# Four residual convolution layers on one core: the first tile's input norm by quarters, the first tile of two later stages by halves and earlier, the last three tiles' offset on another engine

## The chip, the core and the metric

The kernel runs on one core of a Trainium2 chip. A core has five engines that run their own instruction streams in order and wait for one another by semaphores: PE (matrix products into PSUM), DVE (VectorE), ACT (ScalarE), POOL (GpSimd) and SP, which here only issues transfers. Sixteen DMA engines move data between the memory of the chip and the core's own memory. The metric is the device time of one execution in microseconds (us); times of several runs are given by their median. One execution is recorded by the hardware profiler, and all rows below come from it.

## The reference

A batch of 8192 images of 8 channels, 16x16, goes through four layers, each of the form x = x + layer(group_norm(x)) with 4 groups:

```
x = x + L0(_gn(x))   # tensor-train operator of three cores over (8, 16, 16), and a bias
x = x + L1(_gn(x))   # 3x3 convolution, then a batch norm over the whole batch, then relu
x = x + L2(_gn(x))   # 3x3 convolution of values rounded to 8 bits; the scale is the largest |value| of the batch
x = x + L3(_gn(x))   # 3x3 convolution with weights reduced to their sign, edge padding, and a bias
```

L1 needs the mean and variance of its output over the whole batch, and L2 the largest absolute value of its input over the whole batch. So the batch is gone through three times.

## The kernel before

The batch is cut into 64 tiles (NT) of 128 images. A tile is a matrix of 128 partitions (8 channels x 16 rows) by 2048 columns (128 images x 16 columns of a picture) of f32, 1 MB. Three stages follow one another.

**Stage 1** (0 to about 2785 us): layer 0 and the convolution of layer 1. Each tile is loaded twice: as `xb` in a layout whose partitions hold a picture's column and part of the image's number, into one of three buffers `bs`, and as `xt` in the tile layout, into one of four buffers `xs`. The norm of the input works on `xb`: ACT squares it (`norm_b_square`), DVE sums values and squares over rows (`norm_b_sums`), a transpose and five small operations give mean and variance (`group_stats`; its last step, a power of -0.5, is on POOL), a second transpose spreads the result (`norm_b_spread`), and DVE subtracts and multiplies into a buffer `xn` (`norm_b_apply`). Then PE multiplies by the third core (`expand`: tile `pu`, copied to `u` by ACT, two halves for each quarter of a tile) and by the product of the first two cores (`main`: tile `po`, one for each quarter; DVE then adds `po` to `xs`, which is called a drain here). The product of the first two cores is itself made once at the start: POOL spreads the first core into `c0x`, PE makes `cps`, ACT copies it to `core`. `add_bias` adds layer 0's bias to `xs` on POOL. After that come the norm and convolution of layer 1 for the tile before. A loop over the 256 quarters (`for n in range(NT * NQ)`) calls all of this; small constants for later layers (`late_constants`) are made by DVE between the first quarters. The small pack of constants (232 KB) and the large one (690 KB) are loaded from ACT's queue.

PSUM tiles `po`, `pm` and `pc` share three buffers (tag `mm`), so a new one waits until the one three before it has been drained.

**Stage 2** (about 2786 to 3230): for each tile the batch norm and relu of layer 1's output on ACT, `y`, its addition to `x` on POOL (`sum2`), squares on ACT (`square2`), sums by PE (`sums2`, tile `gs`), statistics on DVE and ACT (`stats2`), the power on POOL (`sigma2`), the statistics as rows for PE (`spread2`, tile `gb`), the subtraction of the mean on DVE and the store of the tile (`centre2`), and the running maximum (`range2`). `load2` loads `y` and `x` of a tile; the buffers of a tile's `y` are those of an earlier tile's, so a load waits until that tile's addition has read it. The first four tiles never leave the core's memory. In this stage and the next, tile i is the i-th in the stage's own order. The calls stand in one loop over i, in which tile i is at `sum2`, tile i-1 at `square2`, i-2 at the statistics and i-3 at `centre2`.

**Stage 3** (about 3231 to the end): layers 2 and 3. For a tile: scaling to 8 bits on DVE (`scale2`, `v`), conversion on ACT (`round2`, `q`), PE's convolution in two halves (`layer2`, tiles `pq`); half 0 is drained by DVE after `bias2` added the bias on ACT, half 1 by ACT into `ys` or `z` and an addition on POOL. Then squares (`square3`), sums by PE (`s`), statistics and power (`stats3`), rows (`rows3`, `rows_e`), PE's spreading (`ps_r` the factor, `ps_o` the offset), scaling on DVE (`scale3`), the split into a high part on ACT (`high3`, `hi`) and a low part on POOL (`low3`, `lo`), each with its edge columns copied by ACT (`edges`), PE's convolution of both (`layer3`, tiles `pf`, 24 matmuls), and DVE's last step (`finish`) before the store. `offset3` makes `c`, the offset with the bias, on ACT, and `low3` adds it to `x` on POOL after the low part. A loop over i calls these with shifts, so that tiles i-3 to i+3 are in work together.

**What sets the order.** PE, DVE, ACT and POOL are used through a wrapper that keeps the program's order on each engine; it records all of these instructions at its own line, L43, so that a row is told by its tiles and not by its line. `nc.sync.dma_start` stands outside it: SP issues in the order that the tile framework builds, and it waits in that order.

The rows name what they write and read (out<-in).

Of the kernel before, what the change touches and what calls it, by code (L numbers as in the profile page):

```python
# [8 lines left out]
F32 = mybir.dt.float32  # L9
F32R = mybir.dt.float32r  # L10
BF16 = mybir.dt.bfloat16
# [7 lines left out]
P = 128  # L19
# [4 lines left out]
R = 8  # L24
# [29 lines left out]
def tile_net(ctx: ExitStack, tc: tile.TileContext, xb, xt_in, pack0, pack1, out):  # L54
# [11 lines left out]
    def load_pack(src, parts, pool, name):  # L66
        t = pool.tile([P, src.shape[1]], F32, name=name)
        nc.scalar.dma_start(t, src)
        views, at = {}, 0
        for key, n in parts:  # L70
            views[key] = t[:, at:at + n]
            at += n
        return views
# [209 lines left out]
    with first as s:  # L283
# [24 lines left out]

        def add_bias(t):
            v = samples(T[t]["x"])  # L310
            pool.tensor_tensor(v, v, bias0_t.unsqueeze(1).to_broadcast([P, P, W]), ALU.add)

# [22 lines left out]

        def norm_b_apply(t, q=None):
            src = T[t]["xb"]
            if q in (None, 0):
                T[t]["xn"] = xns[t % 2]
            xn = T[t]["xn"]  # L340
            n = NB // 2 if q is None else NB // NQ
            for k, op, i in ((0, ALU.subtract, src), (1, ALU.mult, xn)):
                for a in range(0, NB, n) if q is None else [q * n]:
                    cols = slice(a, a + n)
                    dve.tensor_tensor(rows_b(xn)[:, cols], rows_b(i)[:, cols],
                                      spread0[:, k, cols].unsqueeze(2).to_broadcast([P, n, 32]), op)

# [147 lines left out]

        load_b(0)
        for t in range(min(3, NT)):
            if t + 1 < min(3, NT):
                load_b(t + 1)
            load_t(t)  # L500
        rest = late_constants(s.enter_context(tc.tile_pool(name="late", bufs=1)))
        next(rest)
        norm_b_square(0)
        norm_b_sums(0)
        c0x = ys[0][:, 0:C * C * H].rearrange("p (n m h) -> p n m h", n=C, m=C)
        pool.tensor_tensor(c0x, w0["c0"].rearrange("p (n m) -> p n m", n=C).unsqueeze(3).to_broadcast([P, C, C, H]),
                           shz[:, 1:H + 1].unsqueeze(1).unsqueeze(1).to_broadcast([P, C, C, H]), ALU.mult)
        norm_b_stats(0)
        cps = ps_u.tile([P, 2 * C, H * R], F32, name="cps", tag="pu")
        for n in range(C):  # L510
            pe.matmul(cps[:, n], c0x[:, n].rearrange("p m h -> p (m h)"), w0["c1"], start=True, stop=True)
        c01v = core01.rearrange("p s (n h) -> p n h s", n=C)
        for n in range(0, C, C // 2):
            act.copy(c01v[:, n:n + C // 2], cps[:, n:n + C // 2].rearrange("p n (h s) -> p n h s", s=R))
        if NT > 1:
            norm_b_square(1)
        norm_b_spread(0)
        for q in range(NQ):
            norm_b_apply(0, q)
            if q == 0:  # L520
                expand(0, 0, 0)
                expand(0, 0, 1)
                add_bias(0)
        if NT > 1:
# [140 lines left out]
    with tc.tile_pool(name="p2", bufs=2) as p2, tc.tile_pool(name="ps2", bufs=2, space=PSUM) as ps2:  # L665
# [14 lines left out]
        nc.vector.tensor_tensor(L["corr"], L["corr"], ksum, ALU.subtract)  # L680

        def sum2(i):
            x, y = T[i]["x"], T[i].pop("y")
            act.activation(y, y, AF.Relu, bias=bn_b, scale=bn_a)
            pool.tensor_tensor(x, x, y, ALU.add)

        def square2(i):
            T[i]["sq"] = p2.tile([P, F], F32, name=f"sq2_{i}", tag="sq2")
            act.activation(T[i]["sq"], T[i]["x"], AF.Square)

# [58 lines left out]
        for i in [*range(STAY), *range(BEGUN, free)]:  # L749
            on(i, load2)  # L750
        for i in range(NT + 4):
            if i == 1:
                on(free, load2)
            on(i + AHEAD2, lambda i: i <= free or load2(i))
            on(i, sum2)
            on(i - 2, sums2)
            on(i - 3, spread2)
            on(i - 1, square2)
            on(i - 2, stats2)
            on(i - 3, centre2)  # L760
            on(i - 2, sigma2)
            on(i - 3, range2)
# [18 lines left out]
    with ExitStack() as s:  # L781
# [53 lines left out]
        def round2(i):  # L835
            q = wk.tile([P, F], BF16, name=f"q_{i}", tag="q")
            act.copy(q, T[i].pop("v"))
            T[i]["q"] = q

        def bias2(i):  # L840
            x = halves(T[i]["x"])[:, 0]
            act.activation(x, x, AF.Identity, bias=L["bias2"], scale=1.0)

        def layer2(i, h):
# [6 lines left out]
            pc, x = pc.rearrange("p k n -> p (k n)"), halves(T[i]["x"])[:, h]  # L851
            if h == 0:
                dve.scalar_tensor_tensor(x, pc, inv, x, ALU.mult, ALU.add)
            else:
                z = z3[i % 2]
                act.activation(z, pc, AF.Identity, bias=L["bias2"], scale=inv)
                pool.tensor_tensor(x, x, z, ALU.add)
# [4 lines left out]
        def stats3(i):  # L862
# [4 lines left out]
            stats_pow(T[i]["mv"])  # L867

        def offset3(i):
            T[i]["c"] = small.tile([P, P], F32, name=f"c_{i}", tag="c")  # L870
            act.activation(T[i]["c"], o3, AF.Identity, bias=L["bias3"], scale=1.0)

        def scale3(i):
            x = T[i]["x"]
            t = t3[i % 2]
            for a, b in HALVES:
                dve.tensor_tensor(samples(t)[:, a:b], samples(x)[:, a:b], over_w(r3, a, b), ALU.mult)
            T[i]["t"] = t


# [8 lines left out]
        def low3(i):  # L889
            hi = T[i]["hi"]  # L890
            T[i]["lo"] = lo = wk.tile([P, P, W + 2], F32R, name=f"lo_{i}", tag="lo")
            pool.tensor_tensor(lo[:, :, 1:W + 1], samples(T[i].pop("t")), hi[:, :, 1:W + 1].bitcast(F32), ALU.subtract)
            x = samples(T[i]["x"])
            pool.tensor_tensor(x, x, over_w(T[i].pop("c"), 0, P), ALU.add)

        def edges3(i):
            edges(T[i]["lo"])

        def layer3(i, h):
            pc = ps_c.tile([P, 2, BANK], F32, name=f"pf_{i}_{h}", tag="pc")  # L900
            for m, t in enumerate(("hi", "lo")):
                for k in range(2):
                    q = 2 * h + k
                    tv = T[i][t][:, q * QS:(q + 1) * QS]
                    for n in range(3):
                        pe.matmul(samples(pc[:, k]), L["sign3"][:, n], tv[:, :, n:n + W],
                                  start=(m == n == 0), stop=(m == 1 and n == 2))
            T[i]["pf", h] = pc

# [14 lines left out]
        for i in range(-FIRST, NT + 4):  # L924
# [4 lines left out]
            at(i, square3)  # L929
            at(i + 1, layer2, 0)  # L930
            spread(i + FIRST, i - 1)
            at(i - 1, offset3)
            at(i + 1, layer2, 1)
            at(i + FIRST, scale2)
            at(i, stats3)
            at(i - 1, scale3)
            at(i - 2, edges3)
            at(i + 2, round2)
            at(i - 1, high3)
            at(i + 2, bias2)  # L940
            at(i - 1, low3)
            at(i - 2, layer3, 0)
            at(i - 2, finish, 0)
            at(i - 2, layer3, 1)

# [63 lines left out]
```

## Time and profile before

| | us |
|---|---|
| three runs, median | 4006.31 (4005.77 to 4006.53) |
| the profiled execution, its own time | 4004.3 |
| its span, first to last instruction | 4002.5 |
| mean granted TensorE clock | 0.963 of full speed |
| PE, DVE, ACT, POOL busy | 3771.8, 3386.6, 2380.6, 2580.2 |
| data moved | 564.48 MB |

The profile gives the busy time of each engine, a picture of the span in 40 slices, the chain of work that ended last (followed back from the last instruction to what released it), groups of instructions, and, for any window, a timeline of instructions with the idle time ahead of each and what ended it. A busy PE is not a PE at its peak, since matmuls are pipelined. Idle time of an engine off the chain costs nothing. By the 40 slices the DMA engines move 390 to 425 GB/s from slice 29 to 32, that is in stage 2, and 95 to 190 GB/s elsewhere.

### The profile page before, as it was taken

What the parts mean: (1) busy time and instruction counts of PE and PEld (TensorE: products, weight loads), DVE (VectorE), ACT (ScalarE), POOL (GpSimd) and SP (SyncE); (2) the same over time, 40 slices, a digit from 0 to 9 for tenths busy, and PEclk for the clock granted to TensorE, in tenths of its full rate; (3) what the DMA queues carried; (4) which work ended last, traced back from release to release, by engine and by line L of the source; (5) the groups of instructions that cost most, each with busy time, mean ns of one, the idle gap of its engine ahead of it and who ended that gap; (6) DMA issues with size and microseconds to landing.
All of it is one profiled execution on the core that took longest, in us unless ns stands there. A gap on an engine that the chain in (4) does not pass through costs nothing.

```text
span 4002.5 us, 55803 instructions
## 1 busy us (share of the span) xinstructions
PE 3771.8 (94%) x20296; PEld 2012.8 (50%) x20358; DVE 3386.6 (85%) x6311; ACT 2380.6 (59%) x2420; POOL 2580.2 (64%) x2597
## 2 busy tenths in 40 slices
PE   8999999999999999999999999998665569999998
PEld 4555555555555555555555555554221135555555
DVE  8888888888888888888888888885999889999997
ACT  4555555555555555555555555554665557777775
POOL 4555555555555555555555555544887759999999
PEclk9999999999999999999999999999777689999999
DMA  3222222222222222222222222213999914444432
GB/s 146 95 95 106 95 95 106 95 95 106 95 95 104 97 95 101 101 95 97 104 95 96 105 95 95 95 54 136 390 424 425 399 42 189 180 179 189 180 148 105
DMA packets 77458, 564.48 MB, mean 141 GB/s; under 512 B 8576, under 2 KB 8704, under 8 KB 8832
## 3 DMA queue, kind: packets, MB, share of 16 engines
q1 hardware_dynamic: 76896, 559.97, 35.8%
q8 instruction: 161, 2.64, 0.3%
q14 instruction: 113, 0.93, 0.1%
q10 hardware_dynamic: 288, 0.94, 0.1%
HBM read 314.47 MB, written 246.42 MB: 140 GB/s over the span
## 4 chain that ended last, share of the span: by engine, by line
PE 86%; DVE 6%; DMA 4%; issue 2%; POOL 1%; ACT 0%; POOLq 0%; DVEq 0%; SPq 0%; ACTq 0%
PE po L43 46%; PE pu L43 14%; PE pf L43 9%; PE pm L43 6%; PE pq L43 4%; PE s L43 3%; PE pc L43 3%; DVE top L43 2%; DMA yk<-y_d 1%; DMA x_d<-u 1%; DMA u<-x_d 1%; DMA x_d<-xs 0%; DMA xs<-x_d 0%; DVE u L43 0%; POOL xs L43 0%
## 5 line engine op out<-in xcount | busy, mean ns | idle before, releaser
L43 PE MATMUL po<-u,core 128*128 128x512 f32 (+1 forms) x4112 | 1895.6, 604 | 1.3 <-DVE xs L43 1.3
L43 ACT COPY u<-pu 128x2048 f32<-128x2048 f32 x512 | 955.6, 1866 | 773.1 <-PE pu L43 773.1
L43 PEld LDWEIGHTS po<-u,core 128*128 128x128 f32 x4112 | 739.8, 190 | 904.5 <-issue 870.4
L43 POOL TENSOR_TENSOR e<-x1n,x 128x512 f32<-128x512 f32 x250 | 302.4, 1209 | 574.7 <-ACT x L43 568.3
L43 PE MATMUL pu<-w,xn 32*128 32x256 f32 x8192 | 587.8, 401 | 4.9 <-DVE xn L43 2.8
L43 DVE TENSOR_TENSOR xs<-po,xs 128x512 f32<-128x512 f32 x256 | 177.1, 692 | 399.4 <-PE po L43 399.4
L43 PEld LDWEIGHTS pu<-w,xn 32*128 32x128 f32 x8192 | 370.4, 184 | 244.6 <-issue 196.0
L43 POOL TENSOR_TENSOR mv<-mv,mhalf 128x4 f32<-128x4 f32 x127 | 129.6, 1020 | 440.7 <-DVE mv L43 440.7
L43 POOL TENSOR_TENSOR v<-e 128x128 f32<-128x128 f32 x750 | 403.1, 552 | 0.0
L43 ACT ACTIVATE m<-pm,b 128x128 f32<-128x128 f32 x250 | 91.9, 368 | 442.6 <-PE pm L43 442.6
L43 PEld LDWEIGHTS pm<-v,fast 128*128 128x128 f32 x2000 | 262.6, 192 | 119.6 <-issue 119.6
L43 POOL TENSOR_TENSOR xs<-xs,w 128x2048 f32<-128x2048 f32 x64 | 291.3, 4553 | 0.0
L43 PE MATMUL pm<-v,fast 128*128 128x128 f32 x2000 | 263.5, 275 | 0.0
L43 ACT ACTIVATE x<-x1n 128x512 f32<-128x512 f32 x500 | 245.3, 542 | 0.0
L43 PE MATMUL pf<-hi,sign 128*128 128x512 f32 x768 | 226.8, 433 | 0.0
L43 PE MATMUL pf<-lo,sign 128*128 128x512 f32 x768 | 219.5, 423 | 3.3 <-ACT lo L43 3.3
L43 POOL TENSOR_TENSOR v<-r 128x128 f32<-128x128 f32 x500 | 219.3, 461 | 0.0
L43 POOL TENSOR_TENSOR mvb<-mvb,mhalf 128x4 f32<-128x4 f32 x64 | 65.2, 1019 | 228.7 <-DVE mvb L43 228.7
L43 ACT ACTIVATE sq<-xs 128x2048 f32<-128x2048 f32 (+1 forms) x107 | 199.1, 1861 | 4.6 <-POOL xs L43 4.6
L43 PE MATMUL gb<-rows_c,sel 128*128 128x128 f32 x128 | 40.4, 409 | 169.8 <-DVE rows_c L43 169.8
L43 PE MATMUL pq<-q,band 128*128 128x480 bf16 (+1 forms) x706 | 188.2, 387 | 10.4 <-ACT q L43 5.2
L43 PEld LDWEIGHTS pf<-hi,sign 128*128 128x128 f32 x768 | 141.4, 191 | 96.6 <-DVE v L43 47.8
(257 smaller groups left out, 6915.3 us busy)
## 6 DMA issues: line engine op xcount, KB each, us to landing
x_d<-xs SPq DMA_DIRECT2D x76, 1024.0 KB, 3.9
bs<-in_xb SPq DMA_DIRECT2D x64, 1024.0 KB, 4.8
xs<-in_xt SPq DMA_DIRECT2D x64, 1024.0 KB, 4.8
y_d<-ys SPq DMA_DIRECT2D x60, 1024.0 KB, 3.9
u<-x_d SPq DMA_DIRECT2D x36, 1024.0 KB, 6.1
xs<-x_d SPq DMA_DIRECT2D x32, 1024.0 KB, 8.9
yk<-y_d SPq DMA_DIRECT2D x29, 1024.0 KB, 19.9
bs<-x_d SPq DMA_DIRECT2D x25, 1024.0 KB, 5.7
```

The costliest lines, as they stand in the source:

```text
L43: return self.tc.keep_in_program_order(op(*args, **kwargs))
```

## The change

Four places of the program are changed. What is computed stays the same.

- **Start of stage 1.** Tile 0's `xb` is loaded by four transfers of 256 KB, and its squares, sums, statistics and application go quarter by quarter (`first_stats`, `first_apply`), with the sums in a cleared corner of a `ys` buffer and two spreading areas in turn. The first two cores' product is made in two halves ahead of it. The large pack's load is placed behind ACT's copies of that product, by the wrapper's order. Layer 0's bias is added by quarters.
- **Start of stage 2.** Tile 0 goes by halves through relu, addition and squares, its addition is on DVE, and the first steps of tiles 0 to 2 stand in a list of their own instead of the loop's order.
- **Start of stage 3.** Tile 0's conversion goes by halves, its second half of layer 2 is drained by DVE like the first (with `bias2` on both halves), and its scaling and high part stand ahead of the next tile's layer 2.
- **End of stage 3.** For the last three tiles there is no `c` and no addition on POOL; `offset_late` adds the offset and the bias on DVE in two halves, behind `scale3`. The last tile's low part and its edges go by halves, and its 24 matmuls stand as high, high, low, low.

In the order that the framework builds for SP, two transfers at the start of stage 2 change places with it: before, the first store of a finished tile (`x_d<-xs`) stands ahead of the load `ys<-y_d` that waits for tile 3's addition; after, behind it, and the same with the next store and load.

```diff
     def load_pack(src, parts, pool, name):
-        nc.scalar.dma_start(t, src)
+        act.dma_start(t, src)
...
+        def first_stats(q):
+            cols = slice(q * NQB, (q + 1) * NQB)
+            for k, src in enumerate((T[0]["xb"], sqs[0])):
+                dve.tensor_reduce(first_sums[:, q, k, 0:NQB], rows_b(src)[:, cols], AX.X, ALU.add)
+            T[0]["mvb", q] = small.tile([P, 2, 2], F32, name=f"mvb_0_{q}", tag="mvb")
+            group_stats(T[0]["mvb", q], first_sums[:, q], W, f"b0_{q}")
+
+        def first_apply(q):
+            spread, cols = spreads[q % 2], slice(q * NQB, (q + 1) * NQB)
+            group_spread(spread, T[0].pop(("mvb", q)), W)
+            xb, xn = rows_b(T[0]["xb"])[:, cols], rows_b(xns[0])[:, cols]
+            for k, op, i in ((0, ALU.subtract, xb), (1, ALU.mult, xn)):
+                dve.tensor_tensor(xn, i, spread[:, k, 0:NQB].unsqueeze(2).to_broadcast([P, NQB, 32]), op)
...
-        load_b(0)
+        T[0]["xb"], T[0]["xn"] = bs[0], xns[0]
+        pool.memset(first_sums, 0.0)
+        for q in range(NQ):
+            cols = slice(q * BANK, (q + 1) * BANK)
+            nc.sync.dma_start(bs[0][:, cols], xb[0][:, cols])
+            act.activation(sqs[0][:, cols], bs[0][:, cols], AF.Square)
...
         for q in range(NQ):
-            norm_b_apply(0, q)
+            first_stats(q)
+            first_apply(q)
             if q == 0:
                 expand(0, 0, 0)
                 expand(0, 0, 1)
-                add_bias(0)
+                if NT > 1:
+                    norm_b_square(1)
+            else:
+                add_bias(0, q - 1)
+        add_bias(0, NQ - 1)
...
         def sum2(i):
             x, y = T[i]["x"], T[i].pop("y")
-            act.activation(y, y, AF.Relu, bias=bn_b, scale=bn_a)
-            pool.tensor_tensor(x, x, y, ALU.add)
+            for xv, yv in pieces2(i, x, y):
+                act.activation(yv, yv, AF.Relu, bias=bn_b, scale=bn_a)
+                (dve if i == 0 else pool).tensor_tensor(xv, xv, yv, ALU.add)
...
-        for i in range(NT + 4):
-            if i == 1:
-                on(free, load2)
+        for f, i in ((sum2, 0), (square2, 0), (sums2, 0), (load2, free), (sum2, 1), (stats2, 0), (sigma2, 0), (square2, 1),
+                     (sum2, 2), (spread2, 0), (sums2, 1)):
+            on(i, f)
+        for i in range(3, NT + 4):
             on(i + AHEAD2, lambda i: i <= free or load2(i))
             on(i, sum2)
-            on(i - 2, sums2)
-            on(i - 3, spread2)
+            if i > 3:
+                on(i - 2, sums2)
+                on(i - 3, spread2)
...
+        def on_dve(i, h):
+            return h == 0 or i == 0
...
         def offset3(i):
+            if i >= LATE:
+                return
...
+        def offset_late(i):
+            x = samples(T[i]["x"])
+            for a, b in HALVES:
+                dve.scalar_tensor_tensor(x[:, a:b], over_w(o3, a, b), L["bias3"], x[:, a:b], ALU.add, ALU.add)
...
+            first = i == 1
+            if not first:
+                at(i + 1, layer2, 0)
             spread(i + FIRST, i - 1)
             at(i - 1, offset3)
+            if first:
+                at(0, scale3)
+                at(0, high3)
+                at(i + 1, layer2, 0)
             at(i + 1, layer2, 1)
             at(i + FIRST, scale2)
             at(i, stats3)
-            at(i - 1, scale3)
+            if not first:
+                at(i - 1, scale3)
+            at(i - 1, lambda j: j >= LATE and offset_late(j))
             at(i - 2, edges3)
             at(i + 2, round2)
-            at(i - 1, high3)
+            if not first:
+                at(i - 1, high3)
             at(i + 2, bias2)
             at(i - 1, low3)
...
```

`LATE` is NT - 3; `pieces2` gives two halves for tile 0 and the whole tile otherwise; `over_w` repeats a row's value over the picture's columns.

## The prediction

> **What bounds the kernel now.** I read the table of stretches first, then the chain that ended last, then the timeline wherever a stretch begins or ends. Columns of the table: stretch, its length, then busy time (and instructions) of PE, its weight loads, DVE, ACT and POOL, the granted TensorE clock, the DMA share and GB/s.
>
> ```profile
> 31.70:2781.00 2749.30, 2747.82 (x15244) 1480.89 (x15244) 2273.59 (x4431) 1530.33 (x1643) 1487.36 (x2191) 1.00 0.25 96
> ...
> 2810.00:3190.00 380.00, 229.30 (x1140) 72.56 (x1140) 352.34 (x540) 226.44 (x227) 314.06 (x114) 0.71 1.01 422
> ...
> 3282.00:3965.00 683.00, 679.66 (x3369) 399.62 (x3425) 631.61 (x1119) 531.64 (x473) 667.17 (x237) 1.00 0.45 170
> ```
>
> Here the reader sees three long bodies that the change leaves alone: the first stage is full on PE (idle 1.5 of 2749.3 us), the second on the DMA engines (share 1.01), the third on PE and POOL (679.7 and 667.2 of 683). Only the start, the two joints and the end can move, and they count only as far as the next body begins or ends at another time. So there are four terms.
>
> ```profile
> 0.72 5.63 DMA bs<-in_xb
> 6.38 4.61 DVE sumb L43 x4
> 20.82 4.72 PE po L43 x16
> ...
> 2788.89 13.52 POOL xs L43 x3
> ...
> 3265.67 4.27 POOL lo L43
> ...
> 3986.73 4.24 POOLq L1004
> 3991.57 4.88 PE pf L43 x18
> ```
>
> These are pieces of the chain (start, us, what): the whole-tile load and its sums at the start, POOL's three adds at the first joint, tile 0's lo on POOL at the second, the last tile's lo (its time stands under POOL's queue) and pf in the tail. The change touches all four places.
>
> **Term 1, the start.** Before, tile 0's load lands at 6.38, sums and small operations run to 13.8, pu follows at 15.37 and po at 20.75; DVE ends tile 0's norm at 19.1. In the new order each quarter costs DVE two reductions of 128x512 (.67, .68), a transpose .24, a reduction .22, then .17, .16, .16, POOL's power (taken .7: .55 with one column, 1.03 with four), the spreading .26 and two applications of .69. With the pitches of the last tile's quarters (2768.41 on) that is 4.97 us a quarter. When does the first quarter land? The DMA engines' row of this stretch adds up to .43 MB at 3.5 us and .63 at 4.0; the quarter and the small pack are .5 MB; with a little for the landing 4.2 (bounds 3.6 and 6.5, where the pack landed before). The first po then starts near 15.5, 5.3 earlier. But DVE ends the norm at 4.2 + 4 x 4.97 + .3 = 24.4, which is 5.3 later, and DVE has no room to spare:
>
> ```profile
> 60.09 0.69 DVE L43 TENSOR_TENSOR xs<-po,xs 128x512 f32<-128x512 f32 x1 [3.79 <-PE po L43]
> ...
> 90.63 2.84 PE L43 MATMUL po<-u,core 128*128 128x512 f32 x6
> ```
>
> In the timeline (start, us, engine) the bracket is the idle time ahead of a drain and who ended it. Up to 60.09 DVE idled for PE .64 + .48 + .48 + 3.79 = 5.39 us (drains at 31.71, 41.26, 50.67, 60.09), which just takes up the 5.3. So this drain stays at 60.1. Then 28.6 us of DVE work follow without a choice (29.6 less one idle of .99) up to the end of the drain that ended at 90.38: now 89.4. The po at 90.63 takes that drain's PSUM buffer, so PE's lead of 5.3 is cut to 1.0 there and stays 1.0 through a stage in which PE is full. Taken -1.0; bounds -3 (quarters of 4.5 us, busy time without pitches) and +1.2 (first landing at 6.5). At nothing I cost: core products and copies by halves (ready near 10, needed by po at 15.5), the large pack after them (690 KB, first read at 32.3), tile 1's square ahead of two u copies (1.91, under DVE's lag) and POOL's bias by quarters (4.54 in all, first needed by the drain at 31.71); without DVE's lag the square alone would cost 1.2.
>
> The row of 5.63 us for 1 MB, shared with two packs, decides the landing. The Trainium skill ("DMA: Bandwidth & Descriptors", section on the anatomy of one DMA) puts one DMA at about 2.0 us plus bytes over 436 GB/s; by that estimate 256 KB issued at .72 land at 3.3, and the term would be -1.9. Its 4.4 us for 1 MB lies below the row, so the row is kept.
>
> **Term 2, the first joint.** The stream of the second stage waits until POOL is through:
>
> ```profile
> 2803.33 4.57 POOL L43 TENSOR_TENSOR xs<-xs,ys 128x2048 f32<-128x2048 f32 x1
> ...
> 2807.05 0.32 SPq L728 DMA_DIRECT2D x_d<-xs  x1
> ...
> 2807.93 0.32 SPq L95 DMA_DIRECT2D ys<-y_d  x1
> ```
>
> The DMA engines stand still from about 2802.5 to 2807 and are full afterwards, so what counts is when SP issues. Tile 0's add goes to DVE (two halves of about 1.2, by rows of 128x1024 such as 2.33/2, while POOL is idle). On ACT relu 0 (2.04), two squares of .95 and relu 1 (2.04) end at 2793.4, no sooner than POOL used to be free for add 1; it stays at 2793.45 to 2798.0, power 0 to 2799.0. Now square 1 stands before relu 2 on ACT, and square 1 waits for add 1: 2798.0 + 1.91 + 2.1 = 2802.05. POOL idles 3 us; add 2 ends 2806.65, add 3 2811.2 (before 2807.90), power 1 2812.25, add 4 2816.8 (before 2813.41). Tile 0 itself is centred at 2805.1 instead of 2807.0. But on SP the load ys<-y_d, whose buffer add 3 must free, now stands in front of tile 0's store, and the next such load in front of tile 1's. SP goes in order, so what left at 2807.05 leaves at 2811.2, the second group at 2816.8 instead of 2812.88, and every transfer of the stage is queued behind them. The full stream moves by 3.9; taken +3.8. Bounds: +4.5 (a further gap between the groups) and -4.3 (the store leaves when the centring can start, 2802.75, and the order on SP does no harm).
>
> **Term 3, the second joint.** For tile 0, q comes in halves (1.90 becomes .95 ahead of pq), and the second half of pq is drained by DVE (1.28) instead of ACT (1.20) and POOL (2.35), with one more bias of 1.15 on ACT. By the rows of 3233.39 on, tile 1's q comes 4.5 earlier and power 0 2.2; scaling 0 and hi 0 (2.34 and 1.93), pulled ahead, could be ready 7 earlier. But POOL takes power 1 before lo 0, and ACT's copy of tile 2's second pq half now stands behind hi 0 (2.47), so the add and power that follow come later on their own chain: lo 0 at 3263.65 instead of 3265.67. From there POOL paces (4.28 + 3.70 + 2.43 + 1.03 = 11.44 of 11.55 us a tile). Taken -2.0; bounds -5 (power 1 keeps the lead of q 1) and 0.
>
> **Term 4, the tail.** The offsets of tiles 61 to 63 leave POOL (3.70 each) and ACT (.35) for two DVE operations of 128x1024; the nearest rows are scaling (1.17) and finish (1.28), so 2.45 a tile. On POOL only the one in front of the last lo held anything up (lo waited from 3986.05, hi's end, to 3986.68). On DVE each stands before the next tile's rows: rows 62 and the sums behind them come 1.8 late, scaling 62 at 3976.2, lo 62 at 3980.5 (before 3978.81); after the second offset scaling 63 at 3984.4 (before 3980.59), hi 63 to 3988.7, lo 63 in halves to 3990.85 and 3993.0 (before in one, to 3990.96). PE has then seven groups of six matmuls at 1.6 us from 3985.4 on: end at 3996.6 to 3997.9 against 3996.45. Taken +0.6; bounds -1.5 (the two offsets hidden, lo's halves alone) and +2.0 (each insertion kept whole on the last tile).
>
> The rows of 2.34 and 2.56 us a tile set the price of the offset on DVE. The Trainium skill ("GPSIMD Engine Reference", key points) holds the DVE to be about twice as fast on elementwise work; by it a tile would take 1.85, by estimate, and the term would be -0.6.
>
> **The sum** is -1.0 + 3.8 - 2.0 + 0.6 = +1.4. The profiled execution took 4004.3 (its span 4002.5 and 1.8 around it), so 4005.7 in such an execution; the median of the runs shown lies 2.0 above it, which gives 4007.7, told as 4007.5.
>
> **Rivals.** (a) The gains hold: DVE's lag does not cut the lead (-5.3) and SP's order does no harm (-4.3): 4006.3 - 5.3 - 4.3 - 2.0 + 0.6 = 3995.3. For it speak POOL's 13.52 us and the long wait for the first load; against it the 5.39 us of DVE idle time, all the room there is, and ACT's order. Chance .15. (b) Slower: POOL's first quarter of the bias add waits for the tile's load of in_xt and stands in front of the third quarter's power, which is due at 4.2 + 2 x 4.97 + 1.7 = 15.8. If that load lands late, DVE and everything behind it slip. Before, it had landed by 13.40, where POOL's add began, which speaks against it; three more issues of .43 us on SP speak for it. A landing at 16.8 takes the start's gain, each further us adds one; with +2.4 from the other terms it needs 22.4 to be 8 us slower: 4014.5. Chance .09. (c) The bodies swallow the start and the second joint, the first joint still pays: 4006.3 + 3.8 + 0.6 = 4010.7. For it: POOL and PE are both full from 3282 on; against it: each body starts when its first tile is ready. Chance .06.
>
> **How the numbers follow.** The forecast has the remaining .70. What a measurement of this kernel can tell from no change is .2%, 8 us: faster is below 3998.3, slower above 4014.3; the forecast and (c) lie between, so .15, .76 and .09. The terms' bounds add up to -13.8 and +7.7 (3992.5 to 4014.0), which would need all four at an end; the range is 3995 to 4013, with half of (a) and all of (b) outside, .16.
>
> **What would show it.** Start: the first po near 15.5, the drain at 60.1 and the one ending at 89.4; if PE does not wait there, term 1 is wrong. First joint: add 3's end near 2811 and SP's first store right behind a load; if the store leaves at 2805, term 2 is wrong and its sign turns. Second joint: lo 0 2.0 closer to the stage's start. Tail: scaling 61 to the last pf .2 to 1.5 us longer than 31.4.

## The result, and the profile after

| | before | after |
|---|---|---|
| median of 6 runs | 4006.03 (4004.99 to 4006.53) | 4008.99 (4007.19 to 4009.74) |
| the profiled execution, its own time | 4004.3 | 4009.25 |
| its span | 4002.5 | 4007.5 |

The ratio is 1.0007, with a 95% interval of 0.9994 to 1.002: no change that this measurement can tell, as forecast (4007.5, range 3995 to 4013). The medians lie 3.0 us apart and the two profiled executions 5.0. The table of stretches of the changed kernel, each stretch moved with its stage, has the columns of the one before: length, busy time (and instructions) of PE, weight loads, DVE, ACT and POOL, granted clock, DMA share, GB/s.

```profile
31.70:2781.00 2749.30, 2746.46 (x15225) 1482.74 (x15223) 2277.21 (x4436) 1528.14 (x1642) 1490.92 (x2193) 1.00 0.25 96
2814.00:3194.00 380.00, 228.44 (x1138) 72.63 (x1137) 351.84 (x537) 225.67 (x226) 312.61 (x114) 0.71 1.01 422
3287.00:3970.00 683.00, 679.92 (x3374) 400.36 (x3426) 631.72 (x1120) 531.68 (x472) 667.17 (x237) 1.00 0.44 170
```

The three bodies are as before: PE full (2.8 us idle instead of 1.5), the DMA engines full (1.01), PE and POOL full. The chain that ended last shows what stands between them (start, us, what):

```profile
0.72 3.66 DMA bs<-in_xb
...
2794.01 4.50 POOL xs L43
2802.51 6.85 POOL xs L43 x2
...
3270.87 4.24 POOL lo L43
```

The first load is on the chain for 3.66 us instead of 5.63. At the first joint POOL's adds are still there, but torn apart: one at 2794.01, and the next two only from 2802.51 on. Three marks cut the span: the bias of the batch norm, written by DVE when stage 1 is over (`bn_b`), POOL's reduction of the maximum when stage 2 is over (`gm`), and the start of tile 0's `lo` in stage 3.

| part of the span | before | after | difference | predicted |
|---|---|---|---|---|
| to `bn_b` | 2786.52 | 2787.03 | +0.5 | -1.0 |
| `bn_b` to `gm` | 444.15 | 448.50 | +4.35 | +3.8 |
| `gm` to tile 0's `lo` | 35.00 | 35.31 | +0.3 | -2.0 |
| tile 0's `lo` to the end of the span | 736.83 | 736.66 | -0.2 | +0.6 |

Only the second line carries a time that counts. The first has to be read with care: in the eight profiles of this document that have the old first stage, one code, `bn_b` stands anywhere from 2786.52 to 2790.42. The start, in the timeline (start, us, engine, what, and in the bracket the idle time ahead and who ended it):

```profile
4.48 0.69 DVE L43 TENSOR_REDUCE ys<-bs 128x16 f32<-128x512 f32 x1 [2.42 <-DMA bs<-in_xb]
...
11.24 1.03 ACT L43 COPY core<-cps 128x512 f32<-128x512 f32 x1 [2.23 <-PE cps L43]
...
12.32 2.09 PE L43 MATMUL pu<-w,xn 32*128 32x256 f32 x16 [1.12 <-ACT core L43]
...
24.51 0.69 DVE L43 TENSOR_TENSOR xn<-xn,stat 128x512 f32<-128x512 f32 x1
...
90.71 5.40 PE L43 MATMUL po<-u,core 128*128 128x512 f32 x8 [2.79 <-DVE xs L43]
```

The quarter is read at 4.48 and the norm ends at 25.2. The line of 90.71 is the step on which the first term stood: PE waits there 2.79 us for DVE's drain and loses its lead. The first joint:

```profile
2794.01 4.50 POOL L43 TENSOR_TENSOR xs<-xs,bs 128x2048 f32<-128x2048 f32 x1 [7.40 <-ACT bs L43]
...
2802.51 4.53 POOL L43 TENSOR_TENSOR xs<-xs,bs 128x2048 f32<-128x2048 f32 x1 [3.02 <-ACT bs L43]
2807.00 4.56 POOL L43 TENSOR_TENSOR xs<-xs,ys 128x2048 f32<-128x2048 f32 x1
2811.58 0.32 SPq L95 DMA_DIRECT2D ys<-y_d  x1
2811.99 0.38 SPq L758 DMA_DIRECT2D x_d<-xs  x1
...
2817.09 0.32 SPq L95 DMA_DIRECT2D ys<-y_d  x1
```

POOL idles 3.02 us for relu 2 on ACT, which stands behind square 1; add 3 (of 2807.00) ends at 2811.56, and only then SP issues, first the load and right behind it the store. Before, that store left at 2807.05.

### The profile page after: what moved, and what is told of

It is laid out like the page before. It is cut to its first block, busy times and chain, and to the rows that moved or that the text cites. A ratio compares the mean times of both kernels' runs of the same rounds, so it can differ in the third digit from the quotient of the medians.

```text
span 4007.5 us, 55850 instructions
## 1 busy us (share of the span) xinstructions
PE 3774.8 (94%) x20296; PEld 2018.7 (50%) x20358; DVE 3401.1 (85%) x6342; ACT 2381.5 (59%) x2424; POOL 2562.4 (64%) x2601
## 4 chain that ended last, share of the span: by engine, by line
PE 85%; DMA 8%; DVE 4%; POOL 2%; issue 1%; ACT 0%; POOLq 0%; SPq 0%; DVEq 0%; ACTq 0%
PE po L43 45%; PE pu L43 13%; PE pf L43 10%; PE pm L43 5%; PE pq L43 4%; PE s L43 3%; PE pc L43 3%; DMA ys<-y_d 2%; DMA xs<-x_d 1%; DMA x_d<-bs 1%; DMA bs<-x_d 1%; POOL bs L43 1%; DMA xn<-x_d 1%; DMA yk<-y_d 0%; DMA x_d<-u 0%
## 5 line engine op out<-in xcount | busy, mean ns | idle before, releaser
L43 POOL TENSOR_TENSOR xs<-xs,w 128x2048 f32<-128x2048 f32 (+1 forms) x67 | 291.4, 4350 | 0.0
L43 POOL TENSOR_TENSOR mvb<-mvb,mhalf 128x4 f32<-128x4 f32 (+1 forms) x67 | 66.9, 999 | 235.2 <-DVE mvb L43 235.2
L43 ACT ACTIVATE sq<-xs 128x2048 f32<-128x2048 f32 (+2 forms) x108 | 199.3, 1845 | 8.2 <-POOL xs L43 5.8
```

The source lines that it names most:

```text
L43: return self.tc.keep_in_program_order(op(*args, **kwargs))
```

## The experiments

Each kernel ran beside the kernel before on the same chip; kernels sent together share those runs. "Stage 2" is the stretch from `bn_b` to `gm` in the kernel's profile. With the first joint as before it took 443.5 to 444.8 us in seven profiles.

**The four parts alone.** Each kernel has one part of the change and is otherwise the kernel before.

Start alone:

```diff
-        load_b(0)
...
+            nc.sync.dma_start(bs[0][:, cols], xb[0][:, cols])
...
+            first_stats(q)
+            first_apply(q)
```

> Only the change at the start, the rest as before. Theory: DVE's longer norm of tile 0 eats PE's lead at the drain near 90 us, so the first stage ends within 1 us of before: -0.5 to +1.0 us in all. Rival: the start brings PE's whole lead of some 2.3 us (po 18.4 instead of 20.75) and the loss lies elsewhere: -2 to -3 us.

Median 4005.48 against 4006.57, ratio 0.9998 (0.9989 to 1.0007). `bn_b` stands at 2786.88, 0.4 later than in the profile before, and PE waits at 90.80 for DVE's drain (1.34 us) as in the full change: no gain that can be told.

First joint alone:

```diff
-            act.activation(y, y, AF.Relu, bias=bn_b, scale=bn_a)
-            pool.tensor_tensor(x, x, y, ALU.add)
+            for xv, yv in pieces2(i, x, y):
+                act.activation(yv, yv, AF.Relu, bias=bn_b, scale=bn_a)
+                (dve if i == 0 else pool).tensor_tensor(xv, xv, yv, ALU.add)
...
+        for f, i in ((sum2, 0), (square2, 0), (sums2, 0), (load2, free), (sum2, 1), (stats2, 0), (sigma2, 0), (square2, 1),
+                     (sum2, 2), (spread2, 0), (sums2, 1)):
+            on(i, f)
```

> Only the change at the first joint. Theory: the whole loss is here, because SP's first transfer behind the standstill leaves some 4 us later (2811 instead of 2807.05): +3.5 to +4.5 us. Rival: the loss needs the other parts, or the second stage gives the late start back: within 1 us of before.

Median 4010.22 against 4006.57, ratio 1.001 (1.0001 to 1.0019), +3.7 us; stage 2 took 449.35. This part alone carries the whole loss. (Its profiled execution, 4014.44, was the slowest of the eleven: in the first stage, whose code is that of before, two copies for `wsum` on DVE took 4.17 instead of 1.35 there, PE waited for DVE, and `bn_b` stands at 2790.42, 3.9 later; 3.1 of it arose there. Stage 2 is counted from `bn_b`, so this is not in the 449.35.)

Second joint alone (`on_dve` and the order of `scale3` and `high3` for tile 0):

```diff
+            if first:
+                at(0, scale3)
+                at(0, high3)
+                at(i + 1, layer2, 0)
```

> Only the change at the second joint. Theory: POOL takes power 1 ahead of lo 0, and power 1 is not earlier, so nothing is gained: -0.5 to +0.5 us. Rival, the prediction's term: -2.0 us.

Median 4004.65 against 4006.57, ratio 0.9998 (0.9989 to 1.0007). The profile shows no gain: tile 0's `lo` starts 34.98 us after `gm` (35.00 before) and the rest is 737.07 long (736.83). The -1.9 of the medians has no counterpart in it and stays unexplained.

Tail alone (`offset_late` for three tiles, the last `lo` by halves):

```diff
+        LATE = NT - 3
...
+            for a, b in HALVES:
+                dve.scalar_tensor_tensor(x[:, a:b], over_w(o3, a, b), L["bias3"], x[:, a:b], ALU.add, ALU.add)
```

> Only the change in the tail. Theory: two offsets of 2.47 us in front of the rows on DVE cancel the 3.7 us off POOL: -0.5 to +0.7 us. Rival: the tail gains by the last low part in halves, -1.5 us.

Median 4007.37 against 4006.57, ratio 1.0004 (0.9995 to 1.0012). Tile 0's `lo` to the end took 739.35, 2.7 longer than in the full change, which has the same code there. Two rows of the timeline of this kernel say where most of it arose:

```profile
3972.81 1.94 PE L43 MATMUL s<-bs,wsum 128*32 128x512 f32 x8
3974.52 1.73 PE L43 MATMUL s<-sq,wsum 128*32 128x512 f32 x8
```

In the full change these sixteen matmuls (3977.28 and 3978.16) took 1.07 and 1.04, 1.6 less. The granted clock was .56 in those 3.5 us here and 1.00 there; a second stretch at half clock follows from 3986.14 on, in `pf` matmuls. The last section comes back to it.

**Which half of the first joint's mechanism?** Two repairs of the kernel with the first joint alone. The first takes away POOL's wait for ACT and leaves SP's order:

```diff
-        for f, i in ((sum2, 0), (square2, 0), (sums2, 0), (load2, free), (sum2, 1), (stats2, 0), (sigma2, 0), (square2, 1),
-                     (sum2, 2), (spread2, 0), (sums2, 1)):
+        for f, i in ((sum2, 0), (square2, 0), (sums2, 0), (load2, free), (sum2, 1), (stats2, 0), (sigma2, 0), (sum2, 2),
+                     (square2, 1), (spread2, 0), (sums2, 1)):
```

> Only the change at the first joint, with the second and third tile's steps swapped back in one place: relu 2 stands ahead of square 1 on ACT, so POOL no longer idles 3 us; SP's order stays as in the changed kernel (loads ahead of stores). Theory: the stage moves by the time of SP's first transfer behind the standstill, here tile 3's addition at about 2808.1 instead of 2811.1: +0.5 to +1.5 us against before. Rival: SP's order alone makes the loss, then it stays at +3.5 to +4.5.

Median 4005.70 against 4006.12, ratio 1.0 (0.9991 to 1.001); stage 2 446.01. Its timeline:

```profile
2795.02 4.50 POOL L43 TENSOR_TENSOR xs<-xs,bs 128x2048 f32<-128x2048 f32 x1 [7.41 <-ACT bs L43]
2800.47 4.54 POOL L43 TENSOR_TENSOR xs<-xs,bs 128x2048 f32<-128x2048 f32 x1
2804.95 4.57 POOL L43 TENSOR_TENSOR xs<-xs,ys 128x2048 f32<-128x2048 f32 x1
2809.55 0.32 SPq L95 DMA_DIRECT2D ys<-y_d  x1
2809.96 0.38 SPq L735 DMA_DIRECT2D x_d<-xs  x1
```

POOL no longer idles between its adds, and load and store leave 3.0 us earlier after `bn_b` (21.5 instead of 24.55). The second repair leaves POOL's wait and puts the stores ahead of the loads on SP:

```diff
-            nc.sync.dma_start(T2[i]["y"], y_d[order2[i]])
+            (sp if i > STAY + AHEAD2 - 1 else nc.sync).dma_start(T2[i]["y"], y_d[order2[i]])
...
-                nc.sync.dma_start(x2_d[order2[i]], x)
+                sp.dma_start(x2_d[order2[i]], x)
```

> Only the change at the first joint, with ACT's order as in the changed kernel (POOL idles 3 us) but SP's order held as before: the store of tile 0 ahead of the load that waits for tile 3's addition, and one load (tile 2's buffer) ahead of it. Theory: the first transfers leave at about 2806.7 and 2808 instead of 2811.1, so the stage is -1 to +1 us against before. Rival: POOL's lag of 3.3 us sets the stage whatever SP does: +3 to +4.

Median 4007.12 against 4006.12, ratio 1.0003 (0.9994 to 1.0012); stage 2 445.78.

```profile
2802.94 4.53 POOL L43 TENSOR_TENSOR xs<-xs,bs 128x2048 f32<-128x2048 f32 x1 [3.03 <-ACT bs L43]
2807.44 4.55 POOL L43 TENSOR_TENSOR xs<-xs,ys 128x2048 f32<-128x2048 f32 x1
2808.68 0.32 SPq L43 DMA_DIRECT2D x_d<-xs  x1
2812.01 0.32 SPq L43 DMA_DIRECT2D ys<-y_d  x1
```

The store leaves 21.2 us after `bn_b`, the load still at 24.55. Each repair brings stage 2 from 449.35 to within 2 us of before, and neither all the way: most of the loss needs both, late adds on POOL and the store behind the load.

**Where does the start's lead go?** If DVE's work near 90 us eats it, taking work away from there must keep it. `late_constants` gets other places:

```diff
-            if n > 0 and q != NQ - 1:
+            if n in (1, 2, 17, 18, 25, 26, 33):
                 next(rest, None)
```

> The change at the start, and the constants for the later layers made by DVE from the 17th quarter on instead of between the 4th and 8th: DVE has 9.5 us less to do between the drains at 61.8 and 90.1. Theory: PE's lead of 2.8 us (pu of the third quarter at 28.96 instead of 31.74) was lost to DVE at 90.7 and is kept now: the first stage ends 2 to 3 us earlier, -2 to -3 us in all. Rival: the lead is lost elsewhere later in the stage: within 1 us of before.

Median 4004.40 against 4006.12, ratio 0.9996 (0.9987 to 1.0005); `bn_b` 2786.32, a miss by the size expected. The drains tell why (start of the same drain in each kernel):

| before | after | this kernel |
|---|---|---|
| 60.09 | 61.77 | 61.77 |
| 89.70 | 89.97 | 85.65 |
| 197.21 | 197.73 | 193.16 |
| 293.97 | 294.49 | 294.81 |

The lead of 4 us now lives past 90 and through to 193. Only part of it is the start's: PE began the first `pu` of tile 0's third quarter at 29.06 instead of 31.74, 2.7 earlier. The rest is a wait that the kernel before has itself, where DVE's constants hold up a drain, and that this kernel has not:

```profile
113.51 3.70 PE L43 MATMUL po<-u,core 128*128 128x512 f32 x8 [1.31 <-DVE xs L43]
```

The lead is lost between 204 and 294, where the constants now stand in blocks of DVE work. PE waits there again in the timeline of this kernel:

```profile
204.46 1.13 PE L43 MATMUL pm<-v,fast 128*128 128x128 f32 x8 [0.58 <-POOL r L43]
216.57 1.13 PE L43 MATMUL pm<-v,fast 128*128 128x128 f32 x8 [1.02 <-POOL mvb L43]
293.31 1.13 PE L43 MATMUL pm<-v,fast 128*128 128x128 f32 x8 [1.12 <-DVE ends L43]
```

So the block was cut: the constants in pieces of at most 1.5 us of DVE time, spread over many quarters.

```diff
-            if n in (1, 2, 17, 18, 25, 26, 33):
+            if n in (1, 2) or (n > 12 and q in (1, 3)):
                 next(rest, None)
...
-        band(wr2, shz, BF16, "2")
-        yield "band 2"
+        yield from band_late(wr2, shz, BF16, "2")
```

`band_late` makes the same band column by column and yields behind each.

> The change at the start, with the later layers' constants cut into pieces of at most some 1.5 us of DVE time and put into DVE's idle places, two for each tile from the fourth tile on (with a scratch of their own). Theory: PE's lead at the drain of the 17th quarter (4.0 us in the run before, 2.8 of it from the start and 1.3 from an old wait) was then lost to the constants that stood there in one block; in pieces they cost nothing: the first stage ends 3 to 4 us earlier, and the time is -2.5 to -4.0 us against before. Rival: the rest of the stage gives the lead back whatever is done: within 1 us.

Median 4001.82 against 4006.16, ratio 0.9987 (0.9978 to 0.9996), -4.3 us; `bn_b` 2783.11, 3.4 earlier than before. No wait of PE for DVE or POOL is left between 34 and 310 us. By the profiles, 1.8 of the 3.4 is the start (the same `pu` at 29.91 instead of 31.74), some 1.4 is the wait at 113.51 that is gone, and from 130 us on PE runs 3.2 ahead, the same in every tile to the last. So the start's lead lives once DVE has room for it, but it is some 2 us and not 3 to 4. The old start with the cut constants was not run, so the two shares are told apart by the profile and not by an experiment. The lead varies, too: the third quarter's first `pu` stands at 31.74 to 33.35 in the eight profiles of the old start and at 28.96 to 30.50 in the six of the new one.

**The tail with one tile.** The offset on DVE for the last tile only:

```diff
-        LATE = NT - 3
+        LATE = NT - 1
```

> The change in the tail for the last tile alone: its offset on DVE and its low part by halves, the offsets of the two tiles before it on POOL as before. Theory: the two offsets in front of the rows on DVE cost what the halves bring; without them the end comes -1.0 to -1.7 us earlier. Rival: POOL's addition in front of the last low part holds it up as before: -0.5 to +0.5.

Median 4005.23 against 4006.12, ratio 1.0 (0.999 to 1.0009). Tile 0's `lo` to the end took 735.19 instead of 736.83: -1.6 in the profile, as expected; the medians can't tell it.

**A better joint.** The idea was to give two adds to DVE and to load earlier than before: adds of tiles 0 and 2 on DVE, add 3 early, and SP held to `x` loads, `y` loads, then stores.

```diff
-                (dve if i == 0 else pool).tensor_tensor(xv, xv, yv, ALU.add)
+                (dve if i in (0, 2) else pool).tensor_tensor(xv, xv, yv, ALU.add)
...
+        for f, i in ((sum2, 0), (sum2, 1), (square2, 0), (sums2, 0), (load2y, free), (spx, free), (spx, free + 1), (sum2, 2),
+                     (spx, free + 2), (sum2, 3), (spy, free + 1), (stats2, 0), (sigma2, 0), (square2, 1), (spread2, 0),
+                     (sums2, 1)):
```

> The first joint, turned towards what counts by the theory, SP's early transfers: tiles 0 and 2 are added on DVE, tiles 1 and 3 on POOL without a wait between, SP takes the loads whose buffers are free first, then tile 3's, then the stores. Tile 3's addition ends near 2801.7 instead of 2807.9 and two loads leave before it. Theory: the second stage is 2.5 to 5 us shorter than before's 443.5 to 444.8. Rival: POOL's later additions (the fifth ends near 2812 as before) set the stage: within 1 us.

Median 4008.79 against 4006.16, ratio 1.0007 (0.9998 to 1.0016); stage 2 447.82: a miss.

```profile
2797.17 5.21 POOL L43 TENSOR_TENSOR xs<-xs,ys 128x2048 f32<-128x2048 f32 x1 [1.32 <-ACT ys L43]
2802.31 1.05 POOL L43 TENSOR_TENSOR gnst<-gnst,mhalf 128x4 f32<-128x4 f32 x1
2802.40 0.32 SPq L43 DMA_DIRECT2D ys<-y_d  x1
...
2808.91 0.69 DVE L43 TENSOR_REDUCE s_c<-gs 128x32 f32<-128x512 f32 x1 [4.98 <-PE gs L43]
2812.12 0.32 SPq L43 DMA_DIRECT2D x_d<-xs  x1
```

The load leaves at 2802.40, as meant. But tile 0's power (2802.31) now stood behind add 3 on POOL, so PE's spreading of tile 0 and with it the sums of tile 1 came late, and the first store left only at 2812.12. The gap had moved from the first load to the first store.

**Together.** The new start with the cut constants, this joint and the one-tile tail, the second joint as before; the lines against the kernel before:

```diff
-            if n > 0 and q != NQ - 1:
+            if n in (1, 2) or (n > 12 and q in (1, 3)):
...
-            pool.tensor_tensor(x, x, y, ALU.add)
...
+                (dve if i in (0, 2) else pool).tensor_tensor(xv, xv, yv, ALU.add)
...
+        LATE = NT - 1
```

> The three together: the start with the constants in pieces, the first joint turned towards SP, and the tail's change for the last tile alone; the second joint as before. Theory: the gains add, since three full bodies lie between them: -3 to -4, -2.5 to -5 and -1.0 to -1.7, in all -6.5 to -10.5 us, so the third part of a per cent at most. Rival: PE's clock at the second joint and in the tail, which moved by 2 us between executions of the same code, hides half of it: -3 to -6.

Median 4002.31 against 4006.16, ratio 0.9988 (0.9979 to 0.9997); stage 2 447.32, the joint's fault still in it. Then the joint mended: add 3 behind tile 0's power, and the stores ahead of the `y` loads on SP.

```diff
-                     (spx, free + 2), (sum2, 3), (spy, free + 1), (stats2, 0), (sigma2, 0), (square2, 1), (spread2, 0),
-                     (sums2, 1)):
+                     (spx, free + 2), (square2, 1), (sums2, 1), (stats2, 0), (sigma2, 0), (sum2, 3), (spread2, 0)):
...
-            on(i + AHEAD2, lambda i: i <= free + 1 or (spy(i) if i == free + 2 else load2(i)))
+            on(i + AHEAD2, lambda i: i <= free or (spy(i) if i <= free + 2 else load2(i)))
```

> As the kernel of three parts before, with the first joint set so that no step of tile 0 is late: tile 1's squares and both sums stand ahead of tile 3's relu, power 0 ahead of tile 3's addition on POOL, and SP's stores ahead of the loads that wait. By the rows, tile 0's store leaves some 3 us earlier than before's (17.3 us behind the batch norm's bias instead of 20.5) and tile 3's load at 18.8 instead of 21.4. Theory: the stage's length follows SP's transfers behind the standstill: 441 to 442.5 us instead of 443.5 to 444.8, and the time is -7 to -10 us against before. Rival: the stage's length is set by what follows later and the joint is worth nothing: 443.5 or more, and -5 to -6 us from the start and the tail alone.

Median 3996.07 (3992.80 to 3997.02) against 4006.03, ratio 0.9973 (0.9961 to 0.9984): 10 us faster than before, and 13 below the changed kernel's own median. Stage 2 took 439.63, less than the 441 to 442.5 expected. In the profiles the span is 7.6 shorter: 3.8 of it up to `bn_b`, 4.5 in stage 2 and 0.3 from tile 0's `lo` on, less 1.0 lost between `gm` and `lo`; the profiled execution of before was itself 1.7 faster than its median. The timeline, and below it the first 40 us of stage 2 from `bn_b` on in the tables of this kernel, of before and of after:

```profile
2797.34 4.57 POOL L43 TENSOR_TENSOR xs<-xs,ys 128x2048 f32<-128x2048 f32 x1 [0.76 <-ACT ys L43]
...
2800.24 0.32 SPq L43 DMA_DIRECT2D x_d<-xs  x1
2801.93 0.32 SPq L43 DMA_DIRECT2D ys<-y_d  x1
```

```profile
2782.76:2822.76 40.00, 23.24 (x115) 6.25 (x114) 32.08 (x49) 30.47 (x27) 30.68 (x11) 0.75 0.93 348
```

```profile
2786.52:2826.52 40.00, 24.00 (x116) 6.32 (x114) 24.42 (x42) 30.27 (x25) 36.94 (x13) 0.64 0.82 309
```

```profile
2787.03:2827.03 40.00, 22.56 (x108) 6.70 (x110) 24.45 (x41) 27.99 (x26) 29.99 (x10) 0.67 0.68 254
```

The last two columns are what to read: the DMA share is .93 here, .82 before and .68 after. What is missing to 1, times 40 us, is the idle time at the start of the stage, as a mean of the sixteen engines. The joints differ in it as in the length of the stage:

| kernel | DMA share of the first 40 us | idle | stage 2 | stage 2 less idle |
|---|---|---|---|---|
| before | .82 | 7.2 | 444.15 | 437.0 |
| after | .68 | 12.8 | 448.50 | 435.7 |
| first joint alone | .68 | 12.8 | 449.35 | 436.6 |
| repair of ACT's order | .77 | 9.2 | 446.01 | 436.8 |
| repair of SP's order | .80 | 8.0 | 445.78 | 437.8 |
| first better joint | .73 | 10.8 | 447.82 | 437.0 |
| first combination | .74 | 10.4 | 447.32 | 436.9 |
| mended joint | .93 | 2.8 | 439.63 | 436.8 |

The last column lies between 435.5 and 437.8 in all fourteen profiles, while the length itself goes from 439.6 to 449.4. In this stage, which the DMA engines fill, their idle time at its start comes back as its length, to within some 2 us.

## Why the prediction was right, and where it was not

**The whole.** No change was forecast with .70 of the chance, and it is what was measured. The sum of +1.4 came out at +3.0 in the medians and +5.0 in the profiles: the two gains that it set against the loss were not there. So the total lies nearer to the forecast than its terms do, and the range was wide enough for their misses.

**Term 2, +3.8: right in mechanism and size.** Stage 2 became 4.35 longer, and 5.2 longer with this part alone. Add 3 ended at 2811.56 and the second group's load left at 2817.09, against 2811.2 and 2816.8 as predicted (the stage began 0.5 later than assumed). That both halves are needed, ACT's order and SP's order, is shown by the two repairs, each of which took most of it away. Rival (a)'s half, that SP's order does no harm, has fallen.

**Term 1, -1.0: right in mechanism, mis-sized.** "The po at 90.63 takes that drain's PSUM buffer, so PE's lead of 5.3 is cut to 1.0 there": PE waits there, and what stays is -0.5 to 0 instead of 1.0. Two of its steps failed. The first `po` started at 18.41 and not near 15.5, since the core's product was costed "at nothing": `cps` has the tag of `pu`, so the first `pu` waited for ACT's second copy of it, to 12.32, with its `xn` ready at 10.6. PE's lead at the first `pu` of the third quarter was 2.8 (28.96 against 31.74), not 5.3. And DVE ended the norm at 25.2, not 24.4, and was still 1.7 late at the drain that was to stay at 60.1; one small operation of the first quarter (DVE, 6.32) took 1.29 there instead of .17, and 1.29 to 1.32 in all six profiles of the new start, for a reason that no run shows. The landing was sized well: the first quarter was read from 4.41 on, with 4.2 taken. The Trainium skill's sum ("DMA: Bandwidth & Descriptors", section on the anatomy of one DMA), which the page gives for transfers issued from GpSimd, made 3.3 by the prediction's estimate for this transfer from SP's queue; the measured 4.41 decides. That DVE's work ate the lead is shown by moving and cutting the constants: with the same start, about 2 us of it reached the end of the stage, and 1.4 more came from a wait of the kernel before.

**Term 3, -2.0: wrong.** It was said that power 1, ahead of `lo` 0 on POOL, would leave `lo` 0 at 3263.65. After:

```profile
3257.91 1.06 POOL L43 TENSOR_TENSOR mv<-mv,mhalf 128x4 f32<-128x4 f32 x1 [0.93 <-DVE diag_d L43]
3267.53 2.36 POOL L43 TENSOR_TENSOR xs<-xs,ys 128x1024 f32<-128x1024 f32 x1 [8.56 <-ACT ys L43]
3269.84 1.02 POOL L43 TENSOR_TENSOR mv<-mv,mhalf 128x4 f32<-128x4 f32 x1
3270.84 4.26 POOL L43 TENSOR_TENSOR lo<-sq,hi 128x2048 fp32r<-128x2048 f32 x1
```

The mechanism is right: POOL takes the addition of 3267.53 and power 1 first, and that addition waits for ACT's copy, which stands behind `hi` 0, with POOL idle for 8.56 us although `hi` 0 was finished at 3265.7. Two sizes failed. By the prediction power 0 came 2.2 earlier and `lo` 0 12.0 behind it. Measured, power 0 came 0.8 earlier (0.55 with this part alone), and `lo` 0 12.9 behind it (12.4 alone), against 11.85 in all twelve profiles of the old joint. So what was pulled ahead was given back on POOL's queue, and a little more. Why power 0 gained so little can't be read from these runs: with the old code it stood anywhere from 21.2 to 24.3 us behind `gm`, with PE's clock (last section), and the clock over these 35 us was .71 and .74 in the two profiles of the new joint against .76 to .86. Held against the trend of the old code (21.2 us at .86, 23.2 at .79, 24.1 to 24.3 at .76 to .78), 22.4 at .71 and 22.6 at .74 are early, so the gain of 2.2 may have arisen and been taken by the clock. Whether the new order or chance made the clock lower is open.

**Term 4, +0.6: near.** The offset cost 2.47 us a tile on DVE (2.45 predicted), the last two `lo` came 1.2 later after tile 0's `lo`, and the halves of the last one gave 1.7 back: its second half ends at 3997.45 and the last `pf` 3.8 later, against 5.5 before. Together -0.2; from scaling 61 to the end of the last `pf` it is 31.4 as before, where .2 to 1.5 more had been said. With one tile on DVE instead of three only the gain is left, -1.6, in the one-tile kernel (735.19) and in the first combination (735.20). In the mended kernel, which has the same tail, -0.3 is seen (736.52): the granted clock was .50 there from 3976.73 to 3980.14, and the twelve `pf` matmuls in that stretch took 2.53 and 2.38 where the first combination has 1.82 and 1.71.

**Rival (b)** did not come: POOL's power of the third quarter ran at 17.85 right behind DVE. **Rival (c)**, 4010.7, lies 1.7 above the median and the forecast 1.5 below. It had the start and the second joint bring nothing, and so it was, but not for its reason, that the bodies swallow them. Tile 0's `lo` to the end took 736.6 to 736.9 us in all eight profiles whose stage 3 is that of before, wherever `lo` 0 stood: each us there reaches the end. And the lead of the start, once kept from DVE's backlog, went through the body of stage 1. The gains were lost before the bodies began or, in stage 1, 60 us into it.

## What to carry to other kernels

A first tile made ready sooner is worth only what the next scarce thing lets through: here DVE's backlog, POOL's queue and SP's queue each took a gain back. Cutting the backlog returned it in the first stage, and reordering POOL's and SP's work at the first joint; for the second joint no run tried. Before work is pulled ahead, list for every engine, and for the queue that issues transfers, what will then stand behind it, and keep the instruction that frees a store ahead of the one that waits longest. Where a stage is full on its DMA engines, count their idle time at its start: here it came back almost one for one.

## What the runs showed of the hardware

**PE's clock after short idle times moves the whole by 3 us.** From `gm` to tile 0's `lo` the twelve profiles of the old joint, one code, fall into three groups with the mean granted clock of these 35 us:

| granted clock | `gm` to tile 0's `lo` | profiles |
|---|---|---|
| .86 | 33.0 to 33.2 | both repairs of the first joint, the first combination |
| .79 | 35.0 to 35.1 | before, start alone, tail alone, one-tile tail, first better joint |
| .76 to .78 | 36.0 to 36.2 | first joint alone, moved constants, cut constants, mended joint |

The same six matmuls after the same idle time, in the first repair of the joint and in the kernel with the cut constants:

```profile
3248.58 1.46 PE L43 MATMUL pq<-q,band 128*128 128x512 bf16 x6 [3.14 <-ACT q L43]
```

```profile
3243.24 2.32 PE L43 MATMUL pq<-q,band 128*128 128x512 bf16 x6 [3.14 <-ACT q L43]
```

Before, they took 2.72. The Trainium skill ("TensorE: Matmul & The Clock Gate", Part 1) describes a clock gate with a free-running window of about 3.4 us, half the rate after an idle window, and a point of change that varies from run to run. The traces agree in the step: the granted clock in them is 1.00 or .50 and changes only at multiples of 3.41 us, which lie elsewhere in each execution. They differ in one point, that the window need not be idle altogether. Two steps of each kernel, first the cut constants, then the first repair (the first value behind the length is PE's busy time, the third from the end the granted clock):

```profile
3240.26:3243.67 3.41, 0.43 (x3) 0.19 (x3) 0.91 (x3) 3.41 (x3) 2.13 (x1) 1.00 0.00 0
3243.67:3247.09 3.42, 3.42 (x11) 1.61 (x10) 1.42 (x2) 2.36 (x2) 0.22 (x1) 0.50 0.00 0
```

```profile
3243.82:3247.23 3.41, 1.62 (x9) 0.73 (x8) 3.21 (x3) 1.69 (x2) 0.34 (x1) 1.00 0.02 5
3247.23:3250.64 3.41, 2.06 (x11) 1.18 (x11) 1.22 (x4) 3.41 (x3) 2.01 (x1) 1.00 0.00 0
```

In the first kernel the idle time falls into one step, PE is busy for .43 us of it, and the next step is halved. In the second the same idle time is shared by two steps with 1.62 and 2.06 us of busy time, and the clock stays. Counted over all fourteen profiles from 2750 us on, a step at full clock with less than 1.4 us of busy PE was followed by a halved one each time (488 steps), one with more than 1.7 never (3301); between them it went both ways. So where the joint or the tail falls on these steps, which no kernel here set, decides up to 3 us. The consequence is measured: a single profile can't settle a question of 2 us at this joint or in the tail, which is why the -1.9 of the second joint alone and the +0.8 of the tail alone are left open; the profile of the tail alone has two halved steps there (from 3972.49 and from 3986.14), that of the full change has none.

**An add on POOL that began beside one on DVE took longer.** An add of 128x2048 took DVE 2.36 us in two halves and POOL 4.5 to 4.6 alone. In the first better joint DVE's add, here one whole instruction, took 2.86; it overlapped an add on POOL that had begun before it by 0.7, which took 4.54, and the next one by 0.8, which took 5.21. In the first combination it was the same, 2.85 and 5.21. In the mended one there is only the first overlap, of 0.7, and POOL's adds took 4.53 and 4.57 with DVE's again at 2.85. The Trainium skill ("GPSIMD Engine Reference", section on specifications) names such contention for DVE instructions with two inputs in the core's memory. The 5.21 goes with the overlap; whether DVE's 2.85 does, or comes from the change of form, is not separated.
